# LSTM cell ends of an adjacency network on one core: the last cell operations of a group in channel halves, the input differences of the outer steps at a later place, and the second output of the 320- and 352-column groups at a later place

## The chip, the cores and the metric

The kernel runs on one core of one Trainium2 chip. The metric is the device time of one execution in microseconds. Before the change it is 1836.33 us, the median of three runs (1835.55 to 1836.9).

## The reference, cut to what matters

The input `x` is 128 graphs of 64 nodes with 256 channels. Four layers follow each other, and each adds to `x` what a graph network makes of `relu(layernorm(x))`. The change lies in the first layer. There, two graph convolutions give `h`, and then four LSTMs with window lengths p = 1 to 4 run over `h` one after the other:

```python
for p in range(1, MAX_SKIP + 1):
    nw = Tv // p
    wins = h[:, :nw * p, :].reshape(Bv * nw, p, Hd)
    last = _lstm_last(Wih[p - 1], Whh[p - 1], bih[p - 1], bhh[p - 1], wins)
    idx = jnp.arange(nw) * p + (p - 1)
    h = h.at[:, idx, :].set(last.reshape(Bv, nw, Hd))
```

One step of the LSTM is

```python
g = x_t @ Wih.T + h @ Whh.T + bias
i, f, gg, o = jnp.split(g, 4, axis=-1)
c = jax.nn.sigmoid(f) * c + jax.nn.sigmoid(i) * jnp.tanh(gg)
h = jax.nn.sigmoid(o) * jnp.tanh(c)
```

so a window of length p takes one step without a state and p - 1 steps with one, and the last hidden state is written over the last row of its window.

## The kernel before, in words

**Layout.** `h` lies in SBUF channel-major, in four tiles `hT` of 2048 tokens each. A channel index has two halves of 128 (`KC` = 2). A state `st` holds two blocks of windows, n = 0 and n = 1, of N columns each. N is 512 for p = 1, 2 and 4. For p = 3, where 21 windows don't divide evenly, it is 320 or 352. Two states, s = 1 and then s = 0, make a group, and they take turns: p = 2 has two groups, p = 3 has two (each with N = 320 in s = 1 and N = 352 in s = 0), p = 4 has one.

**A first step** (`first_step`, without a hidden state) computes the gates i, g and o by `gate`: seven products of a 2x2 Strassen scheme on TensorE (L853), copied and added into a gate tile by ScalarE and VectorE (L869, L866), then activated (L862). Its moving operands are columns of `hT` and four differences of them in the small tile `tx`, which `input_sums` makes on GpSimd (L818). `start` multiplies i and g on GpSimd (L900), `squash` is a tanh on ScalarE (L903), `state` writes the hidden state on VectorE (L829).

**An outer step** (`outer_step`, j = 1 to p - 1) computes the gates from the input and the hidden state together by an outer Strassen scheme over the blocks. Four of its seven products, numbered 5, 2, 4 and 3 in their order, are themselves inner Strassen schemes of seven products each: `strassen` (L961). After each inner product `take` reads its PSUM bank (L970 on ScalarE, L972 on VectorE), because the next product of that bank goes on accumulating in it. The other three outer products are direct ones on 512-, 320- or 352-column operands (`direct`, L985), read by `chained` (L994, L996, L999). `T1` to `T4` are the outer differences of operands: `T1` = x(1) - x(0), in two VectorE instructions, one per channel half (L1035); `T3` likewise on VectorE (L1041); `T2` and `T4` on GpSimd (L1038, L1044). `inner_sum(pr, k)` makes the inner differences of product pr on GpSimd (L947).

The cell operations of an outer step come twice, for n = 0 and n = 1: `act` (L1005, ScalarE), `in_times_g` (L1015, GpSimd: i times g), `keep` (L1018, GpSimd: c times f), `plus` (L1021, GpSimd: the sum), `squash` (L1024, ScalarE: tanh of c), and `out` (VectorE), which writes h (L1032), or, in the last step of a window, the columns of `hT` (L1030). `out(0)`, `squash(0)` belong to n = 0, `out(1)`, `squash(1)` to n = 1. What belongs to n = 1 ends inside the next step.

**The order is written out by hand.** Each operation is an event with a time. `tick(s, fn)` sets it s ticks after the start t0 of its outer step, a step is 52 ticks long, and one tick is one product on TensorE: 28 `strassen` and 24 `direct` ones. All events are sorted by time, and each engine executes its own in that order; semaphores hold an instruction until its inputs are there and its output is free. So a tick does not delay anything, it sets the place in the queues. A negative s lies in the step before. `prep` is a `tick` that is not ahead of `st["h_at"]`, the time that the state's hidden output is planned for. Three steps of the kernel have times of their own: `one` is true in the first outer step of a group's first state (j = 1, s = 1), `last` in the last step of a window, and `fin` in the very last outer step of p = 4.

Of the kernel before, what the change touches and what calls it, by code (L numbers as in the profile page):

```python
# [20 lines left out]
def kernel(ctx: ExitStack, tc: tile.TileContext, a: dict, out: bass.AP):  # L21
# [9 lines left out]
    KC = D // P  # L31
# [9 lines left out]
    NL = a["WihT"].shape[0]  # L41
# [20 lines left out]
    def other_end(name, bufs):  # L62
        scope = ExitStack()
        return scope, scope.enter_context(tc.tile_pool(name=name, bufs=bufs, side="right"))

    last, hlast = other_end("hlast", 1)
# [662 lines left out]
    def at(t, fn, *args):  # L729
        events.append((t, len(events), fn, args))  # L730
# [189 lines left out]
    def outer_step(t0, st, j, tags, fin):  # L920

        N, p, blk, B = st["N"], st["p"], st["blk"], {}
        l, H, a, last = p - 1, N // 2, dict(pl[p]), j == p - 1
# [4 lines left out]
        def tick(s, fn, *args):  # L928
            at(t0 + s, fn, *args)
# [116 lines left out]
        one = j == 1 and st["s"] == 1  # L1046
        ok = st["h_at"] + 0.2

        def prep(s, fn, *args):
            at(max(t0 + s, ok), fn, *args)  # L1050

        for c in range(KC):
            tick((-26 if one else -38) + 0.6 * c, T1, c)
        for k, s in ((0, -35), (1, -34), (3, -33)):
            tick(s + 12 * one, inner_sum, 5, k)
        prep(-11, T2)
        prep(-10.9, inner_sum, 5, 2)
        for k, s in ((0, 1), (1, 2), (3, 3)):
# [22 lines left out]
        e = AT["S", 13] + 2.2  # L1081
# [3 lines left out]
        for k, (hc, g) in enumerate(CHAIN):  # L1085
            e = AT["D", 17 + 2 * k] + 2.6
            for n in range(2):
                tick(e + 0.9 * n, act, ("21", "22")[n], g, hc)
        e = AT["D", 19] + 4.2
# [4 lines left out]
        for i, (g, hc) in enumerate(((0, 0), (1, 0), (0, 1), (1, 1))):  # L1094
            tick((51.3, 53.5)[hc] + 0.1 * g if fin else (58.2, 61.2)[hc] + 1.2 * g, act, "12", g, hc)
        e = 56.2 if fin else 63
        for c in range(KC if fin else 1):
            c = slice(c, c + 1) if fin else slice(0, KC)
            tick(e, in_times_g, 1, c)
            tick(e, plus, 1, c)  # L1100
        tick(58.5, out, 0)
        tick(e + (6.5 if last and p < NL else 4.2), squash, 1)
        tick(e + (8.8 if last and p < NL else 6), out, 1)
        st["h_at"] = t0 + e + 6
        return t0 + 52


# [9 lines left out]
    for p in range(1, NL + 1):  # L1117
        pairs = pairs_of(p)
        for k in range(0, len(pairs), 2):
# [21 lines left out]
            for j in range(1, p):  # L1141
                for st in sts:
                    fin = p == NL and j == p - 1 and st is sts[-1]
                    u = t
                    t = outer_step(t, st, j, now, fin)
                    tags = [now[n] for n in ("spare", "11", "21", "12", "22")]
                    now = dict(now)
                    now["22"], now["spare"] = now["spare"], now["22"]
# [101 lines left out]
    with tc.tile_pool(name="pz", bufs=1, reuse_waits="tile") as pz:  # L1250
# [76 lines left out]
        for s in range(2, NS):  # L1327
            f, t0 = First(s, "rest"), GATE * s
# [213 lines left out]
    with tc.tile_pool(name="pc", bufs=2, reuse_waits="tile") as pc, \  # L1542
# [343 lines left out]
        for i in range(NP):  # L1886
            t0, first_, end = PERIOD * i, i == 0, i == NP - 1
# [60 lines left out]
```

## Time and profile before

| what | value |
|---|---|
| median of the runs (three) | 1836.33 us |
| the profiled execution, its own time | 1838.82 us |
| its span in the trace | 1837.1 us |
| TensorE busy in the span | 1802.4 us, 98% |
| VectorE, ScalarE, GpSimd busy | 65%, 54%, 66% |
| granted TensorE clock | 0.999 |
| first steps of p = 1 | from 182 us |
| outer steps of p = 2, 3, 4 | from about 360, 602 and 902 us |
| end of the last outer step | about 1175 us |

A busy TensorE does not say that it is at its peak, since matmuls are pipelined and their ends are modelled. What can be read is where it stands still. Times in the text are microseconds from the start of the span, and one row of the timeline is "start, duration, engine, line, operation, output<-inputs, how many merged", followed in square brackets by the idle time ahead of it and what ended that.

### The profile page before, as it was taken

What the parts mean: (1) busy time and instruction counts of PE and PEld (TensorE: products, weight loads), DVE (VectorE), ACT (ScalarE), POOL (GpSimd) and SP (SyncE); (2) the same over time, 40 slices, a digit from 0 to 9 for tenths busy, and PEclk for the clock granted to TensorE, in tenths of its full rate; (3) what the DMA queues carried; (4) which work ended last, traced back from release to release, by engine and by line L of the source; (5) the groups of instructions that cost most, each with busy time, mean ns of one, the idle gap of its engine ahead of it and who ended that gap; (6) DMA issues with size and microseconds to landing.
All of it is one profiled execution on the core that took longest, in us unless ns stands there. A gap on an engine that the chain in (4) does not pass through costs nothing.

```text
span 1837.1 us, 24418 instructions
## 1 busy us (share of the span) xinstructions
PE 1802.4 (98%) x8532; PEld 1299.3 (71%) x8532; DVE 1196.0 (65%) x2346; ACT 990.8 (54%) x1776; POOL 1211.8 (66%) x1207
## 2 busy tenths in 40 slices
PE   8999999999999999999999999899999999999998
PEld 7987444466566887787466666566444899999997
DVE  6775555565666666666566666778776566666664
ACT  6765666644545545544644444678684444444442
POOL 5898455765766777776677776767354666666663
PEclk9999999999999999999999999999999999999999
DMA  5754300000003000003000000333200110111111
GB/s 149 242 181 174 115 1 0 6 1 9 6 23 115 1 1 1 1 1 113 26 0 1 1 1 30 109 115 115 70 3 1 47 33 26 47 47 47 47 47 35
DMA packets 67498, 91.20 MB, mean 50 GB/s; under 512 B 4784, under 2 KB 57776, under 8 KB 67376
## 3 DMA queue, kind: packets, MB, share of 16 engines
q1 hardware_dynamic: 66928, 89.35, 14.7%
q8 instruction: 68, 1.11, 0.3%
q14 instruction: 54, 0.44, 0.1%
q10 hardware_dynamic: 448, 0.30, 0.1%
HBM read 56.08 MB, written 33.55 MB: 49 GB/s over the span
## 4 chain that ended last, share of the span: by engine, by line
PE 89%; POOL 5%; ACT 2%; issue 2%; DVE 1%; DMA 1%; SPq 0%; POOLq 0%; DVEq 0%; ACTq 0%
PE ps L961 20%; PE ps L985 16%; PE ps L853 14%; PE ps L1672 8%; PE ps L1282 5%; PE ps L1399 4%; PE ps L1759 3%; PE ps L1639 3%; PE ps L454 2%; PE ps L1735 2%; PE ps L464 2%; PE ps L493 2%; PE ps L1769 2%; PE ps L1800 1%; PE ps L700 1%
## 5 line engine op out<-in xcount | busy, mean ns | idle before, releaser
L972 DVE TENSOR_TENSOR gate<-gate,ps 128x512 f32<-128x512 f32 (+2 forms) x360 | 216.7, 603 | 171.9 <-PE ps L961 160.1
L1005 ACT ACTIVATE gate<-gate,lbias 128x512 f32<-128x512 f32 (+2 forms) x288 | 175.7, 653 | 166.9 <-DVE gate L972 84.2
L866 DVE TENSOR_TENSOR gate<-gate,ps 128x512 f32<-128x512 f32 (+2 forms) x162 | 100.7, 640 | 128.7 <-PE ps L853 118.7
L970 ACT COPY gate<-ps 128x512 f32<-128x512 f32 (+2 forms) x144 | 74.9, 520 | 158.8 <-PE ps L961 158.3
L853 PE MATMUL ps<-tx,wih 128*128 128x512 f32 (+2 forms) x276 | 117.9, 544 | 3.0 <-ACT gate L869 2.5
L1615 ACT ACTIVATE h<-x,ln_rn 128x256 f32<-128x256 f32 x128 | 68.0, 592 | 92.8 <-POOL ln_rn L1612 92.7
L1015 POOL TENSOR_TENSOR gate<-gate 128x1024 f32<-128x1024 f32 (+3 forms) x37 | 73.5, 1986 | 63.1 <-ACT gate L1005 63.1
L862 ACT ACTIVATE gate<-gate,lbias 128x512 f32<-128x512 f32 (+2 forms) x108 | 95.7, 886 | 29.0 <-DVE gate L866 28.9
L1672 PE MATMUL ps<-wl,ag 128*128 128x128 f32 x900 | 108.4, 276 | 0.6
L1672 PEld LDWEIGHTS ps<-wl,ag 128*128 128x128 f32 x900 | 104.2, 192 | 3.3 <-ACT ag L1644 2.5
L961 PEld LDWEIGHTS ps<-h,wb 128*128 128x128 f32 x392 | 70.9, 190 | 41.2 <-issue 21.5
L999 DVE TENSOR_TENSOR gate<-gate,ps 128x512 f32<-128x512 f32 (+2 forms) x144 | 80.7, 602 | 21.6 <-PE ps L985 19.6
L961 PE MATMUL ps<-h,wb 128*128 128x256 f32 (+2 forms) x392 | 91.5, 356 | 1.9 <-POOL wb L947 1.3
L853 PEld LDWEIGHTS ps<-tx,wih 128*128 128x128 f32 x276 | 51.5, 190 | 57.1 <-issue 39.7
L818 POOL TENSOR_TENSOR tx<-hT 128x512 f32<-128x512 f32 (+2 forms) x29 | 36.0, 1242 | 79.2 <-PE ps L853 72.6
L869 ACT COPY gate<-ps 128x512 f32<-128x512 f32 (+2 forms) x108 | 59.4, 550 | 52.4 <-PE ps L853 51.8
L1018 POOL TENSOR_TENSOR cell<-cell,gate 128x1024 f32<-128x1024 f32 (+2 forms) x36 | 73.1, 2030 | 19.9 <-ACT gate L1005 19.9
L985 PE MATMUL ps<-hT,wb 128*128 128x512 f32 x160 | 81.7, 592 | 0.0
L900 POOL TENSOR_TENSOR cell<-gate 128x1024 f32<-128x1024 f32 (+2 forms) x36 | 78.1, 2191 | 5.4 <-ACT gate L862 5.4
L985 PE MATMUL ps<-wih,thA 128*128 128x512 f32 (+2 forms) x192 | 79.3, 495 | 0.0
L853 PE MATMUL ps<-hT,wih 128*128 128x512 f32 (+2 forms) x168 | 78.4, 571 | 0.0
L1021 POOL TENSOR_TENSOR cell<-cell,gate 128x1024 f32<-128x1024 f32 (+3 forms) x37 | 75.5, 2041 | 2.9
(333 smaller groups left out, 4981.5 us busy)
## 6 DMA issues: line engine op xcount, KB each, us to landing
xt<-in_x_dram SPq DMA_DIRECT2D x30, 512.0 KB, 4.4
x1d<-xt SPq DMA_DIRECT2D x16, 512.0 KB, 2.9
x<-x1d SPq DMA_DIRECT2D x16, 512.0 KB, 5.0
out_dram<-x SPq DMA_DIRECT2D x15, 512.0 KB, 3.4
W<-wb SPq DMA_DIRECT2D x6, 896.0 KB, 4.1
wb<-W SPq DMA_DIRECT2D x6, 896.0 KB, 4.9
wb<-in_WihT_dram SPq DMA_DIRECT2D x32, 128.0 KB, 3.4
wb<-in_WhhT_dram SPq DMA_DIRECT2D x24, 128.0 KB, 2.8
```

The source lines that it names most:

```text
L853: nc.tensor.matmul(wide(p_[:, :N]), wih_of(p, k, gi), x_, start=first_, stop=True, skip_group_check=True)
L862: nc.scalar.activation(to, r[bank_][:, :N] if bank_ else to, fn, bias=lbias[:, l, m : m + 1])
L866: nc.vector.tensor_add(slot(n, hc), slot(n, hc), r[bank_][:, :N])
L900: nc.gpsimd.tensor_mul(cell[:, n, :, :N], i, g_)
L961: nc.tensor.matmul(B[pr, name][:, g * H : (g + 1) * H], w[:, g, :], d, start=(new and g == 0), stop=(name, k) in (("a", 4), ("b", 3), ("c" ...
L972: nc.vector.tensor_add(to, to, v)
L985: nc.tensor.matmul(to, w, d, start=(pr == 1 and c == 0), stop=(c == 1), skip_group_check=True)
L999: nc.vector.tensor_add(part(m, k), part(m, k), v)
L1005: nc.scalar.activation(v, v, FN[r, g], bias=lbias[:, l, b : b + 1])
L1021: nc.gpsimd.tensor_add(cell(n)[:, c], cell(n)[:, c], gate_(("11", "12")[n], 0)[:, c])
L1282: nc.tensor.matmul(r[name], con["w1"][:, OF[j], g, :], x_, start=new, stop=(name, j) in (("a", 4), ("b", 3), ("c", 2)), skip_group_check=True)
L1672: nc.tensor.matmul(v["g", name][:, p_, :], x_[:, m, ts(p_, P)], wl2[:, OF[j], m, :], start=new and p_ == m == 0, stop=m == 2 and (name, j) ...
```

## The change

It does three things, all in `outer_step`.

- **Ends of groups.** In the last outer step of the group's second state (s = 0), `in_times_g(1)` and `plus(1)` are issued per channel half: half 0 of both, then half 1 of both. Before, only the very last step of p = 4 (`fin`) did so. It concerns four steps: two ends of p = 2 and two of p = 3.
- **Input differences.** `T1` moves from tick -38 to tick -30.5 for its first half, and from -37.4 to -28.9 for its second. `inner_sum(5, 0)`, which reads the first half, moves from -35 to -28, and `inner_sum(5, 1)` and `(5, 3)` from -34 and -33 to -22 and -21. Steps with `one` keep their times. That leaves 13 steps: two of p = 2, six of p = 3, five of p = 4.
- **Second output of p = 3.** In the groups of 320 and 352 columns, `squash(1)` moves from e + 4.2 to e + 5 and `out(1)` from e + 6 to e + 8, where e = 63, in the four steps of p = 3 that are not the last of a window. The planned time `h_at` follows `out(1)`.

```diff
         for c in range(KC):
-            tick((-26 if one else -38) + 0.6 * c, T1, c)
-        for k, s in ((0, -35), (1, -34), (3, -33)):
-            tick(s + 12 * one, inner_sum, 5, k)
+            tick(-26 + 0.6 * c if one else -30.5 + 1.6 * c, T1, c)
+        for k, s in ((0, -23 if one else -28), (1, -22), (3, -21)):
+            tick(s, inner_sum, 5, k)
...
         e = 56.2 if fin else 63
-        for c in range(KC if fin else 1):
-            c = slice(c, c + 1) if fin else slice(0, KC)
+        halves = fin or last and st["s"] == 0
+        for c in range(KC if halves else 1):
+            c = slice(c, c + 1) if halves else slice(0, KC)
             tick(e, in_times_g, 1, c)
             tick(e, plus, 1, c)
         tick(58.5, out, 0)
-        tick(e + (6.5 if last and p < NL else 4.2), squash, 1)
-        tick(e + (8.8 if last and p < NL else 6), out, 1)
-        st["h_at"] = t0 + e + 6
+        squashed, done = (6.5, 8.8) if last and p < NL else (5, 8) if N < 512 else (4.2, 6)
+        tick(e + squashed, squash, 1)
+        tick(e + done, out, 1)
+        st["h_at"] = t0 + e + done
         return t0 + 52
```

## The prediction, on record before the changed kernel was run

> **What bounds the kernel now.** I read the page first: the busy shares, then the shares of the chain that ended last.
>
> ```profile
> PE 1802.4 (98%) x8532; PEld 1299.3 (71%) x8532; DVE 1196.0 (65%) x2346; ACT 990.8 (54%) x1776; POOL 1211.8 (66%) x1207
> ...
> PE 89%; POOL 5%; ACT 2%; issue 2%; DVE 1%; DMA 1%; SPq 0%; POOLq 0%; DVEq 0%; ACTq 0%
> ```
>
> TensorE is the bound. The change adds no product and removes none, so it can gain only where TensorE stands still. The table of busy time by stage says where that is (first column the stretch, then its length, then PE busy):
>
> ```profile
> 490.00:580.00 90.00, 89.65 (x320) 60.41 (x319) 55.10 (x79) 37.90 (x60) 54.49 (x43) 1.00 0.21 71
> 580.00:600.00 20.00, 17.48 (x60) 10.96 (x59) 13.91 (x26) 14.15 (x28) 15.72 (x12) 1.00 0.00 1
> 600.00:720.00 120.00, 119.37 (x640) 100.34 (x639) 80.09 (x152) 56.77 (x120) 86.08 (x93) 1.00 0.00 1
> 720.00:745.00 25.00, 24.83 (x90) 16.10 (x89) 17.59 (x36) 18.52 (x37) 19.85 (x18) 1.00 0.00 1
> 745.00:862.00 117.00, 116.37 (x627) 98.02 (x626) 77.59 (x146) 55.62 (x117) 84.26 (x90) 1.00 0.10 33
> 862.00:905.00 43.00, 42.20 (x114) 20.45 (x113) 24.28 (x41) 27.82 (x43) 29.39 (x21) 1.00 0.08 33
> 905.00:1150.00 245.00, 245.00 (x880) 166.37 (x879) 157.25 (x207) 103.40 (x163) 174.71 (x127) 1.00 0.04 12
> ```
>
> Length minus busy: 2.5 us idle after the end of p = 2 (580 to 600), 0.6 in each group of p = 3, 0.8 after the end of p = 3, nothing in p = 4. With the 0.35 us ahead of 580 that is 5.1 us, 0.28% of the span. The timeline shows what ends the largest:
>
> ```profile
> 578.91 1.34 ACT L1005 ACTIVATE gate<-gate,lbias 128x512 f32<-128x512 f32 x2
> 580.45 1.34 ACT L1005 ACTIVATE gate<-gate,lbias 128x512 f32<-128x512 f32 x2
> 581.87 2.36 POOL L1015 TENSOR_TENSOR gate<-gate 128x1024 f32<-128x1024 f32 x1 [3.88 <-ACT gate L1005]
> 584.31 2.53 POOL L1021 TENSOR_TENSOR cell<-cell,gate 128x1024 f32<-128x1024 f32 x1
> 586.87 1.06 ACT L1024 ACTIVATE gate<-cell 128x1024 f32<-128x1024 f32 x1 [2.85 <-POOL cell L1021]
> 588.74 1.40 PE L853 MATMUL ps<-tx,wih 128*128 128x320 f32 x4 [1.70 <-ACT gate L869]
> 595.57 1.73 PE L853 MATMUL ps<-tx,wih 128*128 128x352 f32 x4 [0.80 <-ACT gate L869]
> ```
>
> The chain: `in_times_g(1)` waits for the activations of both halves, `plus(1)` follows, ScalarE stands before `squash(1)` until 586.87, and behind it in its queue is the copy (L869) for which TensorE waits 1.70 us. A second wait of 0.80 us follows from the same GpSimd queue, which is then occupied without a break (sums, L947, L900) up to the `tx` sum at 595.45.
>
> The second kind of gap lies in p = 3:
>
> ```profile
> 668.47 1.68 POOL L1015 TENSOR_TENSOR gate<-gate 128x704 f32<-128x704 f32 x1 [0.22 <-ACT gate L1005]
> 668.77 1.76 DVE L1035 TENSOR_TENSOR wb<-hT,hT 128x352 f32<-128x352 f32 x1
> 670.85 1.60 DVE L1035 TENSOR_TENSOR wb<-hT,hT 128x352 f32<-128x352 f32 x1
> 672.92 0.90 DVE L1032 TENSOR_TENSOR h<-gate 128x704 f32<-128x704 f32 x1
> 673.73 0.88 DVE L972 TENSOR_TENSOR gate<-gate,ps 128x320 f32<-128x320 f32 x2
> 674.36 0.78 PE L961 MATMUL ps<-h,wb 128*128 128x160 f32 x4 [0.63 <-POOL wb L947]
> ```
>
> TensorE wants the fifth inner product of number 2 at 673.57. It goes on in the bank of the third one, whose `take` is the first of the two L972 at 673.73. It comes late: two `T1` took 1.76 and 1.60 us, then `out(1)` waited for `squash(1)`. The row names GpSimd's L947, but that result is needed only in the next step; I read the releaser as the `take`. The same wait of 0.63 us stands at 818.34.
>
> **What the skill says.** The Trainium skill, "SBUF — State Buffer", section "SBUF: two separate sides", says that VectorE instructions with two SBUF inputs and GpSimd instructions take one shared port pair as an exclusive lock: the later one waits for the whole of the earlier. The trace agrees: `T1` with N = 320 takes 0.49 us at 584.15, where it starts as L1015 ends, and 1.76 us above (N = 352), where L1015 runs until 670.15. `take` has one input in PSUM and stays at 0.47 to 0.49 us beside GpSimd. The skill's "Perfetto Trace Analysis", section "Identifying the Most-Contended Engine", warns that matmul busy share says little of the roofline; so I use the gaps alone.
>
> **The change part by part.** By both instruction orders, TensorE, ScalarE and SP keep theirs. No moved step issues a DMA.
>
> *Ends of groups.* Eight GpSimd instructions more (two into four, four times). Two activations at 578.91 end at 580.25, so half 0 can start 1.6 us before 581.87. A half-size row (128x512) of L1015 and L1021 exists in the last step of p = 4: 1.28 and 1.27 us at the shortest. Four of them and two dependent starts of 0.07: 580.3 + 5.2 = 585.5, against 586.84 now, 1.3 us earlier. The `T1` at 584.15 (a `one` step, not moved) now meets GpSimd's third or fourth half; through the lock it can push it by 0.45. So 0.9 to 1.3; I take **1.1 us**. The wait of 1.70 shrinks by that. The later GpSimd work up to 595.45 moves along, so TensorE's next two waits keep about their size and the 1.1 us stays. Bounds: 0 (the pieces eaten by starts and the lock) to 2.5 (both waits gone). The other three ends get nothing: at 457 TensorE has no gap; at 735 GpSimd would be 0.9 us early, but its second `tx` sum (732.30) is released by TensorE itself; at 882 `out(1)` is behind VectorE work that waits for TensorE until 878.48, with `squash(1)` done at 878.95.
>
> *Differences and second output.* In VectorE's order, `T1` now stands behind the fourth `take` of product 2 and the first L996: its first half ahead of the fifth `take`, its second half after it. `out(1)` of p = 3 goes from behind the second to behind the third `take`. In the step above: the third `take` can run when its product ends (671.95), to 672.5. L1021, without `T1` in its way, ends at 671.9 instead of 672.03, `squash(1)` at 672.7, `out(1)` (0.82 alone, L1032's shortest row, for 640 columns; 0.9 here) at 673.55, fourth `take` 674.0, L996 674.4, `T1` alone (0.5; GpSimd is empty, because its next instruction, `inner_sum(5, 0)`, waits for this very `T1`) 674.9, fifth `take` 675.3. TensorE, not held at 673.57, wants that bank two products of 0.54 us after the fifth's end at 674.1, at 675.2. So 0.63 us of wait becomes 0.1 to 0.2: I take 0.5 saved, twice, **1.0 us**. In the other four moved steps of p = 3 the same sum leaves about 0.1 us of slack: L996 ends 22 ticks into the step, `T1` 0.45 and `take` 0.45 make 23.6 ticks (0.54 us each), and the bank is wanted at tick 24. In the seven steps of 512 columns a tick is 0.86 us, and 0.6 + 0.6 us fit. Bounds: a loss of 1.2 (0.2 us of new wait in each of six steps) to a gain of 1.5 (both waits and the slower restart behind each).
>
> *What waits behind.* On GpSimd, `inner_sum(5, 0)` now waits for `T1`, and the four sums of product 4 are queued behind it. In the step above they ended between 675.4 and 677.9; they move to about 676.0 to 678.3. TensorE uses the first at 679.30. `inner_sum(5, 1)` and `(5, 3)` are needed in the next step. Their duration, 0.5 to 0.75 us, is hidden; without cover it would cost 13 times that. The second half of `T1` meets `inner_sum(5, 0)` at the lock and delays the sixth and seventh `take` by up to 0.6; their banks are next used some six products later. Later `h_at` binds nothing: the state's next step begins 104 ticks on.
>
> Sum: 1838.82 - 1.1 - 1.0 = 1836.7 for the profiled execution, whose time is 2.5 us over the median of the runs. Off the median: **1836.33 - 2.1 = 1834.2 us**. A measurement of this kernel can tell about 0.2% from no change, 3.7 us, so the forecast is "no difference" by that measure, on the fast side.
>
> **The rivals.**
>
> *The group end opens fully.* If GpSimd runs 1.3 us ahead and the sums after it no longer meet `T1` and `out(1)` at the lock (L947 x3 took 2.19 us at 589.41 where three at 0.53, as at 600.11, take 1.6), both waits go, 2.5 us, and p = 3 gives 1.5: 1836.33 - 4.0 = 1832.3. For it: GpSimd is without a break there, so each saving adds. Against it: the second wait follows from L900, which also needs the g activations. Chance 0.18.
>
> *`T1` ahead of the fifth `take` is the new wait (slower).* If GpSimd is busy at tick 21.5, `T1` again takes 1.2 us, the median of its p = 3 rows, or 1.84, that of p = 4. In p = 3 the fifth `take` then ends at 22 ticks + 1.65 us, 0.6 us after its bank is wanted: six times 0.6 and about 0.2 of restart is 4.8. In 512 columns 1.84 + 0.6 against a room of two products, 1.73: 0.7 + 0.2, seven times, 6.3. Less the 1.1 of the ends: 1836.33 + 10 = 1846.3; new waits begin from a `T1` of about 0.55 us in p = 3, and at about 1 us they outweigh the gain. Against it: after `plus(1)` GpSimd has nothing ahead of `inner_sum(5, 0)`. Chance 0.10.
>
> *The edits miss the gaps.* If the releaser at 674.36 really is L947, or `squash(1)` is held by something else, nothing moves: 1836.3 within 1 us. Chance 0.10.
>
> **How the numbers follow.** Forecast case 0.62, within 0.2%, as is the last rival: same 0.72. Fully open: faster 0.18. New wait: slower 0.10. The forecast's own bounds are +1.2 (a loss of 1.2, no gain) and -4.0, rounded out for the slack in L947 to -4.8: 1831.5 to 1837.5. It holds the fully open case and leaves out the slower rival.
>
> **What would show it.** Right: the wait at 588.74 shrinks by about 1 us, the waits at 674.36 and 818.34 to 0.2 or less, `T1` rows of p = 3 near 0.5 for the first half, the stages 600 to 720 and 745 to 862 otherwise as they are. Wrong: a new TensorE wait on VectorE near tick 24, a `T1` over 1 us at its new place, or an idle time at 580 to 600 still above 2 us.

## The result, and the profile after

In 18 runs each, the changed kernel has a median of 1834.81 us and the kernel before one of 1837.63 us. The ratio is 0.9984, 95% interval 0.9978 to 0.9991: 1.6 per mille, some 2.9 us, off the time, where 2.1 us (1.1 per mille) were forecast. It is no difference by the bound of 0.2%, on the fast side. The interval leaves out 1, so the kernel is a little faster (1.7 to 4.0 us).

The profiled spans differ by more, 1837.1 against 1830.3 us, and most of that isn't the change. To separate it I took, in both traces, the same two TensorE products, one shortly ahead of the four LSTMs (L454, at 154.34 us before) and one shortly behind them (L700, at 1187.01), and compared the time between their starts: 1032.67 us before, 1030.01 after. The LSTMs' own products run from 178.70 to 1180.00 us in before's trace. So 2.7 us lie in the LSTMs and 2.6 us ahead of them in the graph part. The other 1.6 us lie behind them: before's trace has a granted clock of 0.93 there (1175 to 1200 us) and after's 1.00, and between 1192.8 and 1196 us products stand up to twice as far apart as in after's (0.213 us instead of 0.113). This **LSTM stretch** serves below as a second measure: it leaves out what the change doesn't touch. It comes from one execution each, but within it the distances of neighbouring products agree between the traces of before and after to 0.04 us, except at the places named below and in shifts of 0.08 to 0.10 us in p = 3 that nearly cancel.

The page of the kernel after, busy shares and the shares of the chain that ended last:

```profile
PE 1799.8 (98%) x8532; PEld 1298.4 (71%) x8532; DVE 1175.5 (64%) x2346; ACT 991.1 (54%) x1776; POOL 1206.3 (66%) x1215
...
PE 91%; POOL 4%; ACT 1%; DVE 1%; issue 1%; DMA 1%; SPq 0%; POOLq 0%; DVEq 0%; ACTq 0%
```

TensorE is still the bound. GpSimd has the eight instructions more. Busy time by stage in the kernel after (stretch, length, then PE busy):

```profile
580.00:600.00 20.00, 18.58 (x68) 11.92 (x67) 12.54 (x23) 14.34 (x27) 16.50 (x17) 1.00 0.00 1
600.00:720.00 120.00, 119.93 (x641) 100.78 (x641) 78.11 (x154) 56.42 (x120) 86.10 (x93) 1.00 0.00 1
720.00:745.00 25.00, 24.98 (x94) 16.84 (x93) 16.48 (x34) 19.35 (x39) 19.53 (x20) 1.00 0.00 1
745.00:862.00 117.00, 117.00 (x628) 98.60 (x628) 75.84 (x151) 54.61 (x115) 83.94 (x90) 1.00 0.13 45
862.00:905.00 43.00, 42.21 (x105) 19.43 (x104) 24.17 (x36) 29.09 (x44) 30.00 (x24) 1.00 0.07 22
```

Idle TensorE goes from 2.5 to 1.4 us after the end of p = 2 and from 0.6 to 0.1 and nothing in the groups of p = 3. The 0.8 us after the end of p = 3 stay. Now the end of p = 2 in the timeline of the kernel after. In this timeline and those below, rows that the argument doesn't need are left out.

```profile
576.34 1.34 ACT L1005 ACTIVATE gate<-gate,lbias 128x512 f32<-128x512 f32 x2
577.75 1.28 POOL L1015 TENSOR_TENSOR gate<-gate 128x512 f32<-128x512 f32 x1 [2.33 <-ACT gate L1005]
577.88 1.34 ACT L1005 ACTIVATE gate<-gate,lbias 128x512 f32<-128x512 f32 x2
579.12 1.27 POOL L1021 TENSOR_TENSOR cell<-cell,gate 128x512 f32<-128x512 f32 x1
580.34 1.27 POOL L1015 TENSOR_TENSOR gate<-gate 128x512 f32<-128x512 f32 x1
581.58 0.48 DVE L1035 TENSOR_TENSOR wb<-hT,hT 128x320 f32<-128x320 f32 x1
581.70 1.49 POOL L1021 TENSOR_TENSOR cell<-cell,gate 128x512 f32<-128x512 f32 x1
583.22 1.06 ACT L1024 ACTIVATE gate<-cell 128x1024 f32<-128x1024 f32 x1 [1.77 <-POOL cell L1021]
585.09 1.40 PE L853 MATMUL ps<-tx,wih 128*128 128x320 f32 x4 [0.62 <-ACT gate L869]
591.91 1.73 PE L853 MATMUL ps<-tx,wih 128*128 128x352 f32 x4 [0.80 <-ACT gate L869]
```

GpSimd's first half piece (577.75) starts as the first pair of activations ends and runs while ScalarE is still at the second pair of activations. `squash(1)` starts earlier, and TensorE's wait falls from 1.70 to 0.62 us. The second wait of 0.80 us is as it was. Last, the third outer step of p = 3 in the timeline of the kernel after:

```profile
668.30 0.79 ACT L1024 ACTIVATE gate<-cell 128x704 f32<-128x704 f32 x1 [2.07 <-POOL cell L1021]
...
668.51 0.49 DVE L972 TENSOR_TENSOR gate<-gate,ps 128x320 f32<-128x320 f32 x1 [0.59 <-PE ps L961]
...
669.12 0.89 DVE L1032 TENSOR_TENSOR h<-gate 128x704 f32<-128x704 f32 x1
...
669.93 0.71 PE L961 MATMUL ps<-h,wb 128*128 128x160 f32 x4
670.33 0.48 DVE L996 TENSOR_TENSOR gate<-gate,ps 128x320 f32<-128x320 f32 x1
670.73 0.52 DVE L1035 TENSOR_TENSOR wb<-hT,hT 128x352 f32<-128x352 f32 x1
671.16 0.48 DVE L972 TENSOR_TENSOR gate<-gate,ps 128x320 f32<-128x320 f32 x1
...
671.70 0.81 PE L961 MATMUL ps<-wih,wb 128*128 128x160 f32 x4
```

The third `take` (668.51) is now ahead of `out(1)`, `T1`'s first half takes 0.52 us, and the product that waited 0.63 us (674.36 before) starts in its turn at 669.93. The seventh product, which goes on in the bank of the fifth and so stands behind the fifth `take` (671.16), starts at 671.70, 0.14 us late, and its second matmul comes another 0.10 us late. No wait is listed for this; the row is only longer, 0.81 us instead of 0.71.

### The profile page after: what moved, and what is told of

Same layout as the page of the kernel before. It is cut to its first block, busy times and chain, and to the rows that moved or that the text cites. A ratio compares the mean times of both kernels' runs of the same rounds, so it can differ in the third digit from the quotient of the medians.

```text
span 1830.3 us, 24404 instructions
## 1 busy us (share of the span) xinstructions
PE 1799.8 (98%) x8532; PEld 1298.4 (71%) x8532; DVE 1175.5 (64%) x2346; ACT 991.1 (54%) x1776; POOL 1206.3 (66%) x1215
## 4 chain that ended last, share of the span: by engine, by line
PE 91%; POOL 4%; ACT 1%; DVE 1%; issue 1%; DMA 1%; SPq 0%; POOLq 0%; DVEq 0%; ACTq 0%
PE ps L961 20%; PE ps L985 17%; PE ps L853 15%; PE ps L1674 8%; PE ps L1284 5%; PE ps L1401 4%; PE ps L1761 3%; PE ps L454 3%; PE ps L1641 3%; PE ps L464 2%; PE ps L1737 2%; PE ps L493 2%; PE ps L1771 2%; PE ps L1802 1%; PE ps L700 1%
## 5 line engine op out<-in xcount | busy, mean ns | idle before, releaser
L972 DVE TENSOR_TENSOR gate<-gate,ps 128x512 f32<-128x512 f32 (+2 forms) x360 | 216.8, 603 | 185.4 <-PE ps L961 174.5
L866 DVE TENSOR_TENSOR gate<-gate,ps 128x512 f32<-128x512 f32 (+2 forms) x162 | 100.8, 641 | 128.6 <-PE ps L853 118.8
L1015 POOL TENSOR_TENSOR gate<-gate 128x1024 f32<-128x1024 f32 (+4 forms) x41 | 74.3, 1812 | 39.7 <-ACT gate L1005 39.7
L869 ACT COPY gate<-ps 128x512 f32<-128x512 f32 (+2 forms) x108 | 59.5, 551 | 53.0 <-PE ps L853 52.4
L900 POOL TENSOR_TENSOR cell<-gate 128x1024 f32<-128x1024 f32 (+2 forms) x36 | 78.2, 2193 | 5.5 <-ACT gate L862 5.5
L1021 POOL TENSOR_TENSOR cell<-cell,gate 128x1024 f32<-128x1024 f32 (+4 forms) x41 | 74.5, 1816 | 3.2
```

The costliest lines, as they stand in the source:

```text
L866: nc.vector.tensor_add(slot(n, hc), slot(n, hc), r[bank_][:, :N])
L900: nc.gpsimd.tensor_mul(cell[:, n, :, :N], i, g_)
L972: nc.vector.tensor_add(to, to, v)
```

## The experiments

The table sets the ratio to the kernel before (95% interval) beside the LSTM stretch. The timed difference is the ratio less 1, times the median of the kernel before, 1837.6 to 1838.1 us.

| kernel | ratio | timed difference, us | LSTM stretch against before, us |
|---|---|---|---|
| after | 0.9984 (0.9978 to 0.9991) | -2.9 | -2.66 |
| ends alone | 0.9997 (0.9989 to 1.0005) | -0.6 | -1.48 |
| differences alone | 0.9997 (0.9989 to 1.0005) | -0.6 | -0.31 |
| second output alone | 0.9996 (0.9988 to 1.0004) | -0.7 | -0.94 |
| after, `one` sums later | 0.9964 (0.9950 to 0.9977) | -6.6 | -5.98 |
| after, `T1` twice | 1.0021 (1.0014 to 1.0028) | +3.9 | +3.88 |
| after, `T1` behind the take | 0.9981 (0.9974 to 0.9987) | -3.5 | -3.39 |
| sums and `squash(1)` later | 0.9962 (0.9949 to 0.9974) | -7.0 | -6.29 |
| sums, `squash(1)`, `T1` later | 0.9961 (0.9947 to 0.9974) | -7.2 | -7.03 |

Where the difference is several microseconds, the two columns agree to 0.8 us. The three parts alone can't be told from nothing by their times, so for them the trace decides. Their stretches add up to -2.73 us, against -2.66 for the whole.

**The ends alone**, on the kernel before:

```diff
+        halves = fin or last and st["s"] == 0
-        for c in range(KC if fin else 1):
-            c = slice(c, c + 1) if fin else slice(0, KC)
+        for c in range(KC if halves else 1):
+            c = slice(c, c + 1) if halves else slice(0, KC)
```

> The kernel before with the channel halves at the group ends alone; differences and second output as before. My theory: the gain of the ends is one end, that of p = 2. TensorE's wait of 1.70 us there falls to about 0.6, the wait of 0.80 after it stays, the two waits of 0.63 in p = 3 stay. 1.2 us less than before, a ratio of 0.9993. Rival, that all four ends gain: waits of TensorE shrink after 735 and 893 too, and the time falls by 2 us or more. Rival, that the halves do nothing without the moved differences: 1.70 stays.

The waits of TensorE in the LSTMs (engine, line, releaser; us in total, times, longest). In the kernel before:

```profile
PE ps L853 <- ACT gate L869: 3.7, 4, 1.7
PE ps L961 <- POOL wb L947: 1.3, 2, 0.6
```

In the kernel after, L947 is gone from this list:

```profile
PE ps L853 <- ACT gate L869: 1.9, 3, 0.8
```

With the ends alone:

```profile
PE ps L853 <- ACT gate L869: 2.6, 4, 0.8
PE ps L961 <- POOL wb L947: 1.2, 2, 0.6
```

The long wait on the copy L869 loses 1.1 us and nothing else in the list moves: the two waits of p = 3 stand. The stretch loses 1.48 us. By the starts of the products, 1.1 us of it is at the end of p = 2 and 0.36 at the end of the first group of p = 3, where the prediction had nothing.

**The later differences alone**, on the kernel before:

```diff
-            tick((-26 if one else -38) + 0.6 * c, T1, c)
+            tick(-26 + 0.6 * c if one else -30.5 + 1.6 * c, T1, c)
-        for k, s in ((0, -35), (1, -34), (3, -33)):
-            tick(s + 12 * one, inner_sum, 5, k)
+        for k, s in ((0, -23 if one else -28), (1, -22), (3, -21)):
+            tick(s, inner_sum, 5, k)
```

> The kernel before with the later differences alone; out(1) of p = 3 stays behind the second take. My theory (the releaser of the p = 3 waits is the third take, held by out(1) behind it on VectorE): the two differences go back to about 0.5 us, but out(1) still stands ahead of the third take and waits for squash(1), which ends 2.7 us after the stretch's fifth D product; the third take ends at about the same time as before less 0.2, so a wait of 0.4 us stays in both groups of p = 3. Rival (the releaser is GpSimd's L947, as the trace names it): L947 leaves that place, so both waits go to zero. Rival (the lock of the differences alone made the take late): both waits go to zero as well, and then e3_out keeps them.

The step of p = 3 in its timeline:

```profile
671.45 0.89 DVE L1032 TENSOR_TENSOR h<-gate 128x704 f32<-128x704 f32 x1 [1.20 <-ACT gate L1024]
672.26 0.88 DVE L972 TENSOR_TENSOR gate<-gate,ps 128x320 f32<-128x320 f32 x2
672.88 0.78 PE L961 MATMUL ps<-h,wb 128*128 128x160 f32 x4 [0.46 <-DVE gate L972]
...
674.11 0.56 POOL L947 TENSOR_TENSOR wb<-wb 128x176 f32<-128x176 f32 x1 [3.52 <-DVE wb L1035]
```

`T1` is out of the way, and VectorE stands 1.20 us before `out(1)` for `squash(1)`, with the third `take` (the first of the two L972) queued behind it. The wait falls only from 0.63 to 0.46 us. Its named releaser is now the `take`; the sums L947, named before, run only after the product has started, so it does not need them.

**The later second output alone**, on the kernel before:

```diff
-        tick(e + (6.5 if last and p < NL else 4.2), squash, 1)
-        tick(e + (8.8 if last and p < NL else 6), out, 1)
-        st["h_at"] = t0 + e + 6
+        squashed, done = (6.5, 8.8) if last and p < NL else (5, 8) if N < 512 else (4.2, 6)
+        tick(e + squashed, squash, 1)
+        tick(e + done, out, 1)
+        st["h_at"] = t0 + e + done
```

> The kernel before with the later squash(1) and out(1) of p = 3 alone; the differences stay where they meet GpSimd at the lock, at 1.6 to 1.8 us each. My theory (the third take waits for out(1)): the third take runs right after the second, at about 672.8, and TensorE's two waits of 0.63 us in p = 3 go to 0.1 or nothing: 1.5 us less than before. Rival (L947 is the releaser): L947 hasn't moved, both waits stay at 0.6. Rival (the differences alone made the take late): both waits stay at 0.4 or more.

The same step in its timeline:

```profile
668.22 1.76 DVE L1035 TENSOR_TENSOR wb<-hT,hT 128x352 f32<-128x352 f32 x1
670.30 1.60 DVE L1035 TENSOR_TENSOR wb<-hT,hT 128x352 f32<-128x352 f32 x1
...
671.82 0.87 DVE L972 TENSOR_TENSOR gate<-gate,ps 128x320 f32<-128x320 f32 x2
672.61 1.09 DVE L1032 TENSOR_TENSOR h<-gate 128x704 f32<-128x704 f32 x1
673.02 0.71 PE L961 MATMUL ps<-h,wb 128*128 128x160 f32 x4
```

`T1` is where it was and as slow as it was (1.76 and 1.60 us, as before), and the wait is gone all the same, since the third `take` now runs ahead of `out(1)`. ScalarE's order is the same as before, so only VectorE's order differs. With the run before this one, that shows the third `take` behind `out(1)` as the cause. The 1.5 us expected did not come: each place wins 0.87 us, but then the sixth and the seventh product start 0.16 and 0.25 us late, with `out(1)`, 1.09 us long here, now ahead of the fourth `take`.

**The sums of the first outer step, later.** On the kernel after, three `inner_sum` of product 5 in `one` steps stand in GpSimd's queue ahead of the last two `tx` sums of the first step that is still running (three L947, 585.76 to 587.95, with the `tx` sum at 587.90 behind them). Here they go behind the last `tx` sum:

```diff
-        for k, s in ((0, -23 if one else -28), (1, -22), (3, -21)):
+        for k, s in ((0, -15 if one else -28), (1, -14.9 if one else -22), (3, -14.8 if one else -21)):
```

> The changed kernel, with the three inner sums of product 5 of each group's first outer step (one) moved from ticks -23 to -21 to ticks -15 to -14.8, behind the last tx sum of the first steps on GpSimd. My theory: the second wait after each end (0.80 us after the end of p = 2, and those of 0.5 and 0.3 after the end of p = 3) is GpSimd's queue: the sums stand ahead of the product of i and g (L900), ScalarE's squash waits for that, and the copy for TensorE stands behind the squash. Moved, L900 starts 1.5 to 2.2 us earlier and these waits go: 2.5 to 3.5 us less than the changed kernel, a ratio to before of 0.9970. Rival: L900 waits for the activations of g, so the waits stay within 0.2 us of the changed kernel's. Rival: the sums come late for the first outer step, and TensorE waits for L947 there.

GpSimd and TensorE in its timeline at the end of p = 2:

```profile
586.33 1.40 PE L853 MATMUL ps<-tx,wih 128*128 128x320 f32 x4 [0.62 <-ACT gate L869]
...
587.22 1.16 POOL L818 TENSOR_TENSOR tx<-hT 128x352 f32<-128x352 f32 x1 [0.18 <-PE ps L853]
588.35 3.04 POOL L900 TENSOR_TENSOR cell<-gate 128x640 f32<-128x640 f32 x2
...
591.36 0.93 POOL L818 TENSOR_TENSOR tx<-hT,tx 128x352 f32<-128x352 f32 x1
592.26 2.19 POOL L947 TENSOR_TENSOR wb<-wb 128x160 f32<-128x160 f32 x3
```

From TensorE's first wait (the row of 0.62 us) to L900 it is now 2.0 us (586.33 to 588.35), against 3.7 in the kernel after (585.09 to 588.80); the three L947 follow behind the last `tx` sum. TensorE's row of this place, in the same timeline, has no wait any more:

```profile
592.19 1.35 PE L853 MATMUL ps<-tx,wih 128*128 128x352 f32 x4
```

In the kernel after that row was 1.73 us long behind its wait of 0.80, because in its middle the weight loads waited again, 0.57 us for the `tx` sum. Both belong to the cost: from the two products ahead of it (0.76 us in their row) to the four behind it is 1.78 us here, and 3.11 in the run with the ends alone, where the row and a wait of 0.79 are as in the kernel after. So this one wait was worth 1.33 us. Counted in the same manner, between the kernel after and this one, the end of the first group of p = 3 gives 0.50 us, though no row there shows a wait of TensorE's, and that of the second 1.32. The sum is 3.15 of the 3.32 us by which the stretch is shorter.

**Each moved `T1` twice**, on the kernel after, to see where the slower rival begins. The second issue repeats the first and computes nothing new:

```diff
-            tick(-26 + 0.6 * c if one else -30.5 + 1.6 * c, T1, c)
+            for _ in range(1 if one else 2):
+                tick(-26 + 0.6 * c if one else -30.5 + 1.6 * c, T1, c)
```

> The changed kernel with each moved difference (T1, both halves, the 13 moved steps) executed twice in a row, which changes no result. It takes the place of the slower rival: what a longer T1 ahead of the fifth take would do. My theory: in the 320-column steps the slack is all but used up, so 0.45 us more ahead of the fifth take is a wait of 0.4 to 0.5 us, plus 0.1 to 0.2 of restart, in each of the four (two ahead of each N = 352 state); the two 352-column steps have about 0.1 to 0.2 us more room and lose 0.3; the seven of 512 columns take 0.6 + 0.6 + 0.6 against 1.73 and lose 0.1 or nothing. In all 2.5 to 3.5 us more than the changed kernel, and the named releaser is VectorE's L972. Rival, that the fifth take isn't the deadline: no new wait, and the time stays within 0.1% of the changed kernel.

Its waits of TensorE in the LSTMs, first line:

```profile
PE ps L961 <- DVE gate L972: 3.8, 13, 0.5
```

And one of the 13 places in its timeline:

```profile
612.15 1.08 DVE L1035 TENSOR_TENSOR wb<-hT,hT 128x352 f32<-128x352 f32 x2
613.14 0.48 DVE L972 TENSOR_TENSOR gate<-gate,ps 128x320 f32<-128x320 f32 x1
613.68 0.81 PE L961 MATMUL ps<-wih,wb 128*128 128x160 f32 x4 [0.42 <-DVE gate L972]
```

All 13 moved steps now wait for the fifth `take`. By the starts of the products, each of the seven 512-column steps loses 0.46 us against the kernel after (0.355 at the product that waits, 0.105 right behind it), four of p = 3 (products of 160 columns) 0.56, and two (176 columns) 0.52. Together that is the 6.5 us between the two stretches, where 2.5 to 3.5 were expected: p = 3 lost 3.3 us, about as reckoned, and the 512-column steps 3.2, where 0.1 us each or nothing was expected.

**`T1` behind the fifth `take`**, on the kernel after:

```diff
-            tick(-26 + 0.6 * c if one else -30.5 + 1.6 * c, T1, c)
+            tick(-26 + 0.6 * c if one else (-29.7, -28.9)[c], T1, c)
```

> The changed kernel with both halves of T1 behind the fifth take (ticks 22.3 and 23.1). My theory: the late matmul starts that the changed kernel's trace shows at the sixth product of the 320-column steps (0.1 to 0.24 us each, four of them) come from the first half of T1 ahead of the fifth take; they go, 0.5 to 0.8 us less than the changed kernel, which timing can hardly tell, but the starts can. Rival (they come from out(1)): they stay.

The late starts of 0.10 to 0.24 us, which the kernel after has in four steps of p = 3, are gone (the product is the seventh; the expectation calls it the sixth), and the stretch is 0.7 us shorter. In the step shown above the seventh product now starts 0.54 us after the sixth instead of 0.68. By its times alone this kernel can't be told from the kernel after. So, by its trace, `T1` ahead of that `take` is a small cost, not a gain.

**`squash(1)` later at the ends of p = 2**, with the sums later:

```diff
-        squashed, done = (6.5, 8.8) if last and p < NL else (5, 8) if N < 512 else (4.2, 6)
+        squashed, done = (9.1, 11.4) if last and p == 2 else (6.5, 8.8) if last and p < NL else (5, 8) if N < 512 else (4.2, 6)
```

> e4_sums, and at the two ends of p = 2 squash(1) goes from tick 69.5 to 72.1 and out(1) from 71.8 to 74.4, behind the copy (L869) that TensorE waits for. My theory: the last wait of the end of p = 2 (0.62 us, 0.8 with its restart) is ScalarE standing before squash(1) with the copy behind it; it goes, 0.8 us less than e4_sums. Rival: GpSimd's tx sums are then the next releaser, and 0.3 us or more of the wait comes back two products later. Rival: out(1), now later on VectorE, meets GpSimd's L900 at the lock and holds the adds behind it: no gain.

The condition holds in all four outer steps of p = 2, those of the first states too; no start of TensorE moves there. Its timeline at that place:

```profile
584.59 0.43 ACT L869 COPY gate<-ps 128x320 f32<-128x320 f32 x1 [0.53 <-PE ps L853]
585.03 1.06 ACT L1024 ACTIVATE gate<-cell 128x1024 f32<-128x1024 f32 x1
...
587.91 1.51 PE L853 MATMUL ps<-tx,wih 128*128 128x352 f32 x4
589.25 1.48 PE L853 MATMUL ps<-hT,wc 128*128 128x352 f32 x4
```

The copy now stands ahead of `squash(1)` and the wait of 0.62 us is gone. The stretch is only 0.3 us shorter than with the sums alone, since the two rows behind it take 1.51 and 1.48 us where such a row takes 1.35: in both, weight loads wait. The stretch wins 0.89 us at the copy and loses 0.55 again, so the 0.8 us expected did not stay. The weight loads' named releasers are a `tx` sum (0.44 us) and VectorE's L866 (0.43 and 0.42), which fits both rivals of the expectation; no run separates them.

**Everything together**, with `T1` behind the fifth `take` as well:

```diff
-            tick(-26 + 0.6 * c if one else -30.5 + 1.6 * c, T1, c)
+            tick(-26 + 0.6 * c if one else (-29.7, -28.9)[c], T1, c)
```

> e7_squash and e6_behind together, the candidate for a version that beats both kernels. If the parts add up: 3.3 (sums) + 0.8 (squash) + 0.6 (behind) = 4.7 us less than the changed kernel, a ratio to the kernel before of 0.996. If the second half of T1 meets GpSimd's sum at the lock and makes the sixth and seventh take late: new waits on VectorE's L972, and no more than e7_squash.

It has the shortest stretch, 7.0 us under before and 4.4 under the kernel after, where 4.7 were expected. Its stage after the end of p = 2, by busy time, has no gap left:

```profile
580.00:600.00 20.00, 20.00 (x74) 12.96 (x73) 13.83 (x27) 16.11 (x31) 19.21 (x18) 1.00 0.00 1
```

The last two kernels, at 1830.15 and 1830.39 us (five runs each), can't be told apart by time. Both beat the kernel before, and the kernel after by about 4 us.

## Why the prediction was right, point by point

- **The sum.** Of the 2.66 us in the stretch, 1.08 lie at the end of p = 2 (forecast 1.1), 1.25 at the two waits of p = 3 (forecast 1.0) and 0.36 at an end where nothing was forecast. So the mechanism came as forecast and the size was 0.6 us too small. That the median, 1834.81 us, is so near the 1834.2 forecast is in part luck: the kernel before has a median 1.3 us higher in 18 runs than in the three that the forecast started from.
- **The bound.** TensorE bounds the kernel: this held. But the gaps counted, 5.1 us, are less than what could be had. The last version gains 7.0 us, because a wait also stretches the products behind it, and a stretched product counts as busy.
- **Ends of groups, 1.1 us forecast.** The wait at the end of p = 2 lost 1.08 us (1.70 to 0.62), and the stretch 1.1 us there. The parts of the sum are in the timeline: L1015 starts once the first pair of activations is done, and `T1` at 581.58 meets the last L1021, which takes 1.49 us instead of 1.27. "The other three ends get nothing" missed 0.36 us at the end of the first group of p = 3. There, with the ends alone, a weight load that waited 0.47 us (735.10 before, GpSimd's L947 named) waits 0.11, and the one that waited 0.64 us for the copy L869 waits 0.51.
- **Differences and second output, 1.0 us forecast.** The two waits of 0.63 us went. Each place won 0.87 us in the starts of the products, more than its wait, and the seventh product then lost 0.24 (forecast 0.1 to 0.2). That is 0.62 us net, where 0.5 was taken. The reading of the releaser as the third `take` is shown by the two runs with one part each. How the gain splits is not what the text suggests, since it names the two slow `T1` first: alone, the later output takes away both waits (0.94 us), the later differences a fourth of each (0.31 us).
- **Slack of the other steps.** About 0.1 us of slack was reckoned in the other four moved steps of p = 3. Two of them (160-column products) start the seventh product 0.10 us late, two (176 columns) don't. The sum took 0.45 us each for `T1` and `take`, which is under the shortest rows of both (0.48 and 0.47); in the two late steps `T1` takes 0.52. In 512 columns the doubled `T1` measures the room: 1.41 us of `T1` and 0.6 of `take` against a room of 1.73 give 0.28, and the waiting product started 0.355 us late. So the forecast that single ones fit was right.
- **What waits behind.** The sums of products 5 and 4 moved without a cost that shows: no TensorE wait on them appears in the list of the kernel after.
- **The rival that opens fully** failed by its mechanism. Its 4.0 us stand at the edge of the measured 1.7 to 4.0, so the time alone would not refute it; the trace does. It expected the second wait to go once GpSimd ran earlier. The wait stayed. L900 was named against this rival, rightly, but with the wrong thing holding it: not the g activations, but three sums of the next outer step ahead of it in GpSimd's queue. Moving those alone brought L900 forward by 1.7 us and took the wait away.
- **The slower rival** needs a slow `T1` at the new place. There it took 0.48 to 0.77 us in p = 3 and at most 0.91 in 512 columns, since GpSimd was empty for the first half. The Trainium skill's exclusive lock ("SBUF — State Buffer", section "SBUF: two separate sides") agrees with what moving `T1` away from GpSimd's instructions did: its medians fell from 1185 to 594 ns (p = 3, first steps included) and from 1840 to 764 ns (p = 4). The lines of `T1`, in the kernel before and then in the kernel after (minimum, median, maximum in ns):

```profile
L1035 DVE TENSOR_TENSOR wb<-hT,hT x16: 486/1185/2242, 584.1 to 814.8; 128x320 f32<-128x320 f32 x8, 128x352 f32<-128x352 f32 x8
L1035 DVE TENSOR_TENSOR wih<-hT,hT x12: 682/1840/1922, 879.1 to 1095.9; 128x512 f32<-128x512 f32 x12
...
L1035 DVE TENSOR_TENSOR wb<-hT,hT x16: 484/594/1158, 581.6 to 814.6; 128x320 f32<-128x320 f32 x8, 128x352 f32<-128x352 f32 x8
L1035 DVE TENSOR_TENSOR wih<-hT,hT x12: 684/764/909, 873.9 to 1097.9; 128x512 f32<-128x512 f32 x12
```

With 1.4 us of `T1` ahead of the `take` in 512 columns and about 1 us in p = 3 the kernel was 3.9 us slower than before. So a `T1` that long does make TensorE wait, and the turning point lies below that; no run here had a `T1` made that long by GpSimd at the new place.

## What to carry to other kernels

Where an engine executes in order, look for what stands ahead of the late instruction in its queue and could stand behind it: the second output ahead of a `take`, a `squash` ahead of a copy, sums of the next step ahead of a `tx` sum. Each was worth 0.3 to 1.3 us in one place, more than making an instruction faster did here (`T1` from about 1.7 to 0.5 us: 0.16 us in one place). When single edits are under what the clock can tell, compare a stretch between the same two instructions in both traces, and check that the parts add up to the whole.

## What was not expected of the hardware

- A TensorE wait costs more than its row says. The wait of 0.80 us at the end of p = 2 was worth 1.33 us, because the four products behind it took 1.73 us instead of 1.35, with weight loads that waited once more. With `T1` twice, the listed waits of 0.19 us in the 512-column steps cost 0.46 each. At the end of the first group of p = 3 0.5 us was lost that no wait of TensorE's shows, in just such a row.
- A named releaser can be one that no one waited for. L947 was named for 0.63 us twice, but with the differences moved the same product started at 672.88, before the first of those sums at 674.11.
- The span of one profiled execution moved by 4.2 us outside the changed code between two kernels, 1.6 of it where before's granted clock is 0.93 over 25 us.
